# A second level of the seven-product scheme inside one block product, and layer statistics from accumulated sums

## The chip, the cores and the metric

The kernel runs on one core of a Trainium2 chip. A core has five engines that run at the same time and wait for each other through semaphores: TensorE (PE) multiplies matrices into PSUM, VectorE (DVE) and ScalarE (ACT) work on elements and can read PSUM, GpSimd (POOL) works on elements in SBUF alone, and SyncE (SP) issues the transfers (DMAs). Each engine works through its own list of instructions in order. The metric is the time of one execution on the device in microseconds (us), less is better. All data are float32.

## The reference

The input x has 128 graphs of 128 nodes with 512 features, and adj is one 128x128 matrix for all. Four layers follow each other, and each ends with the residual and a layer norm over the features:

```python
# --- layer 0: y = adj @ x;  out = y @ W0 + bias
x = _layernorm(x + _L0_gnn_ref(x, adj, weight, bias))
# --- layer 1: rel = adj.T * (q @ k.T), each row divided by its norm;  out = rel @ v
x = _layernorm(x + _L1_gnn_ref(x, adj, Wq, Wk, Wv))
# --- layer 2: attention with softmax of leaky_relu(s1 + s2) * adj;  elu(att @ h + beta * h), h = x @ W
x = _layernorm(x + _L2_gnn_ref(x, W, a, beta, adj))
# --- layer 3: for each node the greatest of relu(...) over the features
x = _layernorm(x + _L3_gnn_ref(x, adj, adj, b))
```

The layer norm is `(x - m) / sqrt(v + 1e-5)` with mean m and variance v of each node's 512 features.

## The kernel before, in words

The 128 graphs are taken in 32 groups g of four. For one group a layer's big product is [512 rows] x [512 x 512 weights]: y @ W0 in layer 0 (written `y`), x @ (Wq.T Wk) in layer 1 (written `m`), x @ Wv.T in layer 1 (`v`) and z @ W in layer 2 (`z`). There are four such products per group. Each is done by a Strassen-Winograd scheme: the operands are cut into 2x2 blocks of 256x256, seven block products P1 to P7 replace eight, and sums of blocks are made before and after. `left_factors` makes the sums of the left operand on POOL (tiles `s_y`, `s_x`, `s_z`), `weight_blocks` makes those of the weights once. A block product is four matmuls of 128x128 weights against 256 columns. A float32 matmul appears in the profile as two records, so a block product has eight.

`product` issues the seven in the order 1, 2, 6, 5, 7, 3, 4. Their sums are formed in PSUM as far as possible, in regions:

```python
ORDER = (1, 2, 6, 5, 7, 3, 4)
REGION = {1: 0, 6: 0, 7: 0, 4: 0, 2: 1, 5: 2, 3: 2}
BLOCK = {1: (0, 0), 2: (0, 0), 6: (0, 1), 3: (0, 1), 5: (1, 1), 7: (1, 1), 4: (1, 0)}
```

P1, P6, P7 and P4 are accumulated onto one another in region 0; after each of them the region's present value is read out (`out`) into the block that BLOCK names, and the next of them can begin only when that read is done. P5 and P3 share region 2 in the same way. P2 is alone in region 1 and is added to block (0, 0). For `m`, `v` and `z` the read-outs of 1, 6, 5 and 4 are copies on ACT, the others adds on DVE. For `y` all read-outs are adds on DVE, and ACT copies the bias into regions 0 and 2 beforehand (`fill`).

Between the block products stand smaller steps of PE, one after each of the first products: `aggregate` (p_y, adj @ x of the next group; ACT copies it to yT) in `m`, `scores` (p_rel) in `y`, `gather` (p_z; ACT copies it to zT) in `v`, and `widen` (p_a, read by DVE for the maximum, `mx`) and `attend` (p_o, read by DVE with the residual) in `z`. In PSUM region 0 has two banks, regions 1 and 2 share one bank, the small steps share three banks (`bank`), and two banks hold a constant (`wa`).

The order of the work is written out by hand. Every step is put on a list with a time (`emit(at, ...)`), where 28 units are one group's period; the list is sorted, and each engine gets its instructions in the order of that list (`keep_in_program_order`). TABLE gives the times of an ordinary group; FIRST and LAST give those of the first two and the last three. Four groups are in work at once. While `y` of group g runs, layer 2 of group g - 2 makes its attention: `leaky` (DVE, two operations on e), `weighted` (POOL, e times adj), `greatest` (DVE, nm), `exps` (ACT) and `divide` (DVE).

The statistics of layers 0, 1 and 2 are made by `stats`, a pair of DVE instructions (BATCH_NORM_STATS2 and BATCH_NORM_AGGREGATE) for each graph. `norm` turns them into scale and shift, and ACT applies these. Layer 3 of the ordinary groups already uses sums and ACT's squares.

All instructions are issued through one helper, so the profile puts them all on line L26. Groups are told apart by the names of their tiles.

Of the kernel before, what the change touches and what calls it, by code (L numbers as in the profile page):

```python
# [8 lines left out]
FP = mybir.dt.float32  # L9
# [20 lines left out]
def kernel(  # L30
# [52 lines left out]
    dram = ctx.enter_context(tc.tile_pool(name="dram", bufs=2, space=bass.MemoryType.DRAM))  # L83

    def bank(name):
        return psum.tile([P, D], FP, tag="ps", name=name, bufs=3)

    def on_all(row, n):

# [27 lines left out]

    w2_sb = const.tile([P, K, D], FP)
    nc.sync.dma_start(w2_sb, w2.rearrange("(k p) f -> p k f", p=P))
    a_sb = data.tile([P, 2, D], FP, tag="x3", name="a_sb")  # L120
    nc.sync.dma_start(a_sb.rearrange("p s d -> p (s d)"), on_all(a2, 2 * D))
    beta_sb = const.tile([P, 1], FP)
    nc.sync.dma_start(beta_sb, on_all(beta, 1))
# [33 lines left out]
    def weight_blocks(at, key, w, keep=0, tag=None):  # L157

        def blk(kh, ch):
            return w[:, 2 * kh : 2 * kh + 2, H * ch : H * ch + H]

        t = {}

        def factor(i):
            if i == 0:
                home, args = (const, {}) if tag is None else (data, dict(tag=tag))
                u = home.tile([P, 3 + keep, 2, H], FP, name=f"t_{key}", **args)
                t.update({2: u[:, 0], 3: u[:, 1], 4: u[:, 2]})  # L170
                t[1] = u[:, 3] if keep else blk(0, 1)
                bw[key] = {
                    1: blk(0, 0), 2: blk(1, 0), 3: blk(1, 1), 4: t[4], 5: t[1], 6: t[2], 7: t[3],
                }
            to, left, op, right = (
                (3, blk(1, 1), ALU.subtract, blk(0, 1)),
                (2, t[3], ALU.add, blk(0, 0)),
                (4, blk(1, 0), ALU.subtract, t[2]),
                (1, blk(0, 1), ALU.subtract, blk(0, 0)),
            )[i]  # L180
            dve.tensor_tensor(t[to], left, right, op)

        for i in range(4):
            emit(at[i], factor, i)

    bw = {}


    def prepare_v(c):
# [7 lines left out]
    def prepare_dots(k):  # L197

        for i in range(2):
            scr = work.tile([P, D], FP, tag="scr", name=f"scr_wa_{i}_{k}", bufs=2)  # L200
            dve.scalar_tensor_tensor(
                scr,
                w2_sb[:, k, :],
                1.0,
                a_sb[:, i, :],
                op0=ALU.mult,
                op1=ALU.mult,
                accum_out=col[:, i, k : k + 1],
            )
# [21 lines left out]
    def row(at, step, n=G):  # L231
# [4 lines left out]
        load=[-20], y=row(0.5, 1), y_sums=row(4.3, 0.5), y_w=row(7, 1, 7),  # L236
        stats0=row(14.4, 0.4), norm0=[16.2], apply0=row(16.8, 0.33),
        turn=row(21.4, 1), turn_blocks=row(18.4, 0.6),
        move=row(20.5, 0.1), x_sums=row(25.3, 0.5), m=row(28, 1, 7), scores=row(36.5, 1),
        masked=[39.95], squares=[40.4], turn_rel=[40.3],  # L240
        move_rel=row(41.2, 0.1), inverse=[42.5], v=row(42, 1, 7), attend=row(50.6, 1),
        residual=row(51.0, 1), dots=[51.7, 53.8, 54.9, 55.6], norm1=[54.6], scale=[57.2],
        apply1=row(65.4, 0.33),
        spread=[57.3], leaky=[62.6], weighted=[62.9], greatest=[63.9], exps=[64.0],
        divide=[65.2], turn_att=[68.6], with_beta=[69.0], turn_blocks_2=[65.7], move_2=[65.8], gather=row(71.5, 1),
        z_sums=row(75.3, 0.5), z_w=row(77, 1, 7), exp=[86.0, 87.0, 96.0, 99.6],
        elu=[86.4, 87.4, 96.8, 100.3], norm2=[101.4], apply2=row(102.4, 0.33),
        widen=[104.2, 104.9, 105.6, 106.3], top=[104.7, 105.4, 106.1, 106.8],
# [53 lines left out]
    REGION = {1: 0, 6: 0, 7: 0, 4: 0, 2: 1, 5: 2, 3: 2}  # L302
    BLOCK = {1: (0, 0), 2: (0, 0), 6: (0, 1), 3: (0, 1), 5: (1, 1), 7: (1, 1), 4: (1, 0)}

    def left_factors(at, s, aT, tag, name, keep):

        def blk(nh, kh):
            return s[aT][:, 2 * kh : 2 * kh + 2, 2 * P * nh : 2 * P * (nh + 1)]  # L310

        def first():
            sums = work.tile([P, 3 + keep, 2, 2 * P], FP, tag=tag, name=f"s_{name}")
            s1, s2, s4 = (sums[:, i] for i in range(3))
            s3 = sums[:, 3] if keep else blk(1, 0)
            s["f"] = {1: blk(0, 0), 2: blk(0, 1), 3: s4, 4: blk(1, 1), 5: s1, 6: s2, 7: s3}
            pool.tensor_tensor(s1, blk(1, 0), blk(1, 1), ALU.add)

        emit(at[0], first)
        emit(at[1], lambda: pool.tensor_tensor(s["f"][6], s["f"][5], blk(0, 0), ALU.subtract))  # L320
        emit(at[2], lambda: pool.tensor_tensor(s["f"][7], blk(0, 0), blk(1, 0), ALU.subtract))
        emit(at[3], lambda: pool.tensor_tensor(s["f"][3], blk(0, 1), s["f"][6], ALU.subtract))

    def by_rows(p, a, b, first):

# [21 lines left out]
                    skip_group_check=True,  # L347
                )

    def product(at, name, mul, s, w, c, fresh, begin=None, before=None, lead=0.7):  # L350

# [26 lines left out]
        def out(i):  # L380
# [3 lines left out]
            else:  # L384
                dve.tensor_tensor(dst, p, dst, ALU.add)

        for n, i in enumerate(ORDER):
            if before is not None and i in (1, 5):
                emit(at[n] - (0.7 if i == 5 else lead), fill, REGION[i])
            emit(at[n], step, i)  # L390
            emit(at[n] + 0.72, out, i)
# [9 lines left out]
        dve.bn_stats(st, t)  # L401
        dve.bn_aggr(s["mv"][:, b, :], st)

    def norm(at, apply_at, s, g, t):

        n = G // len(at)

        def spread(i):
            sl = slice(i * n, i * n + n)
            ve = small.tile([P, n], FP, tag=f"ve{n}", name=f"ve_{g}_{i}")  # L410
            dve.tensor_scalar(ve, s["mv"][:, sl, 1], EPS, None, op0=ALU.add)
            s["r", i] = small.tile([P, n], FP, tag=f"rstd{n}", name=f"rstd_{g}_{i}")
            pool.tensor_tensor(s["r", i], ve, mhalf[:, sl], ALU.pow)

# [23 lines left out]
    def layer0(g, t):  # L438
        s = {}

        def aggregate(b):
# [12 lines left out]
                s["yT"][:, :, b * P : (b + 1) * P], p.rearrange("p (k n) -> p k n", k=K)  # L454
            )

        if g > 0:
            emit(t["load"][0], load, g)
        each(t["y"], aggregate)
        left_factors(t["y_sums"], s, "yT", "s_yz", f"y_{g}", 0)  # L460
        product(
            t["y_w"],
            f"y_{g}",
# [4 lines left out]
            False,  # L468
            before=bias_halves,
            lead=4.4 if g == 0 else 0.7,  # L470
        )
        each(t["stats0"], lambda b: stats(s, f"0_{g}", b, x1[g][:, b, :]))
        norm(t["norm0"], t["apply0"], s, f"0_{g}", lambda: x1[g])
# [1 line left out]

    def layer1(g, t):
        s = {}

# [109 lines left out]
        def residual(b):  # L590
            if b == 0:
                x2[g] = data.tile([P, G, D], FP, tag="x2", name=f"x2_{g}")
            dve.scalar_tensor_tensor(
                x2[g][:, b, :],
                s["o", b],
                s["rn"][:, b : b + 1],
                x1[g][:, b, :],
                op0=ALU.mult,
                op1=ALU.add,
            )  # L600
            if g < NG - 1:
                stats(s, f"1_{g}", b, x2[g][:, b, :])


        def dots(b):
            if b == 0:
                s["d"] = small.tile([P, 2, G], FP, tag="d12", name=f"d12_{g}")
            for i in range(2):
                scr = work.tile([P, D], FP, tag="scr", name=f"scr_{g}_{b}_{i}", bufs=2)
                dve.scalar_tensor_tensor(  # L610
                    scr,
                    x2[g][:, b, :],
# [24 lines left out]
        else:  # L637
            each(t["turn_blocks"], turn_blocks)
            each(t["move"], move)
        left_factors(t["x_sums"], s, "xT", "s_x", f"x_{g}", 1)  # L640
        product(t["m"], f"m_{g}", by_columns, s, "m", middle_block, True, begin_middle)
        each(t["scores"], scores)
        emit(t["masked"][0], masked)
        emit(t["squares"][0], squares)
# [3 lines left out]
        else:  # L648
            emit(t["turn_rel"][0], turn_last)
        emit(t["inverse"][0], inverse)  # L650
        product(t["v"], f"v_{g}", by_rows, s, "v", rows_of(lambda: s["v"]), True, begin_values)
        each(t["attend"], attend)
        each(t["residual"], residual)
        if g == NG - 1:
            each(t["stats1"], lambda b: stats(s, f"1_{g}", b, x2[g][:, b, :]))
        each(t["dots"], dots)
        emit(t["scale"][0], scale_dots)
        norm(t["norm1"], t["apply1"], s, f"1_{g}", lambda: x2[g])

    s12 = {}  # L660

# [3 lines left out]
    def layer2(g, t):  # L665
        s = {}
        late = g >= NG - 2


        def spread():  # L670
# [61 lines left out]
            engine.tensor_tensor(e, e, rs[:, :, None].to_broadcast([P, n, P]), ALU.mult)  # L732

        def turn_att(i):
            if i == 0:
                s["p"] = bank(f"p_eT_{g}")
            for b in range(i * n, i * n + n):
                pe.transpose(s["p"][:, b * P : (b + 1) * P], s["e"][:, b, :], ident)

        def with_beta(i):  # L740
            if i == 0:
                s["eT"] = work.tile([P, G, P], FP, tag="eT", name=f"eT_{g}")
            dve.tensor_tensor(
                s["eT"][:, i * n : i * n + n, :],
                s["p"].rearrange("p (b n) -> p b n", b=G)[:, i * n : i * n + n, :],
                beta_b[:, i * n : i * n + n, :],
                ALU.add,
            )
# [57 lines left out]

        def elu(b):
            if b == 0:
                if g < NG - 1:
                    x3[g] = data.tile([P, G, D], FP, tag="x3", name=f"x3_{g}")  # L810
                else:
                    x3[g] = work.tile([P, G, D], FP, tag="xB", name=f"x3_{g}")
            x = x3[g][:, b, :]
            dve.scalar_tensor_tensor(
                x, s["c", b], 0.0, x2[g][:, b, :], op0=ALU.max, op1=ALU.add
            )
            dve.scalar_tensor_tensor(x, s["m", b], 1.0, x, op0=ALU.min, op1=ALU.add)
            stats(s, f"2_{g}", b, x)

        n = G // len(t["exps"])  # L820
        emit(t["spread"][0], spread)
# [10 lines left out]
            emit(t["move_2"][0], move)  # L832
        each(t["gather"], gather)
        if g < NG - 1:
            left_factors(t["z_sums"], s, "zT", "s_yz", f"z_{g}", 0)
            product(t["z_w"], f"z_{g}", by_rows, s, "2", rows_of(lambda: s["c"]), True, begin)
        else:
            each(t["z_w"], direct)
        each(t["exp"], exp)
        each(t["elu"], elu)  # L840
        norm(t["norm2"], t["apply2"], s, f"2_{g}", lambda: x3[g])

    def layer3(g, t):
        s = {}

        def widen(b):
            s["a", b] = bank(f"p_a_{g}_{b}")
            pe.matmul(s["a", b], adjT, x3[g][:, b, :], start=True, stop=True)  # L850


# [153 lines left out]
```

## Time and profile before

| | |
|---|---|
| median of 3 runs (lowest to highest) | 2173.91 us (2173.57 to 2174.77) |
| the profiled execution | 2173.83 us |
| its span, first to last instruction | 2172.0 us |
| granted TensorE clock | 0.996 |
| PE busy | 2149.1 us, 99% |
| DVE, ACT, POOL busy | 1560.6 us (72%), 1115.4 us (51%), 720.8 us (33%) |
| matmul records of 128x256: mean of one | 379 ns |
| matmul records of 128x128: mean of one | 275 ns |
| BATCH_NORM_STATS2 on DVE | x392, 685 ns |
| BATCH_NORM_AGGREGATE on DVE | x392, 182 ns |
| ACT square of 128x512 with its sum | 620 ns, and 190 ns to read the sum |
| POOL sum of 128x512 | 1270 ns |

The page of a profile gives busy times by engine, the chain of work that ended last, and groups of like instructions with their number, the mean of one, and the idle time before them. Matmuls and DVE and ACT instructions overlap with their successors, so the mean duration of one is longer than the time from one start to the next; the timeline, which lists instructions with their start, shows the latter.

### The profile page before, as it was taken

The page shows a single profiled execution, that of the slowest core. Times are in us where ns is not written, and L with a number is a line of the kernel's source. Part 1 is how long each engine was busy: PE and PEld are TensorE (multiplying, and loading weights), DVE is VectorE, ACT ScalarE, POOL GpSimd, SP SyncE. Part 2 cuts the span into 40 slices and gives each one's busy share as a digit, 9 for nine tenths or more (in the row PEclk, how much of TensorE's full clock was granted, in tenths as well). Part 3 has the DMA queues.
Part 4 walks back from the last instruction along what each step waited for, and adds up shares of the span by engine and source line. Part 5 has one row for each costly group of instructions (what it writes and reads, how often), then busy time and mean ns, then how long its engine had stood idle before and what let it go on. Part 6 is the DMA issues. An engine that isn't in the chain of part 4 may idle for free.

```text
span 2172.0 us, 31973 instructions
## 1 busy us (share of the span) xinstructions
PE 2149.1 (99%) x10887; PEld 1820.3 (84%) x10887; DVE 1560.6 (72%) x3429; ACT 1115.4 (51%) x2470; POOL 720.8 (33%) x589
## 2 busy tenths in 40 slices
PE   9999999999999999999999999999999999999996
PEld 8888888888888888888888888888888888888882
DVE  4667676776777776777777767767777767777677
ACT  3235545555545555455555455554455554555554
POOL 4223333333333233334233233323332333333331
PEclk9999999999999999999999999999999999999998
DMA  4012222322122322222222223222322222332201
GB/s 171 25 37 64 58 72 72 71 54 59 59 76 66 77 55 51 67 73 69 55 58 62 74 71 73 54 56 62 75 67 66 58 56 70 74 68 55 39 20 59
DMA packets 361970, 138.31 MB, mean 64 GB/s; under 512 B 303184, under 2 KB 318672, under 8 KB 361808
## 3 DMA queue, kind: packets, MB, share of 16 engines
q1 hardware_dynamic: 361280, 135.22, 24.8%
q8 instruction: 88, 1.44, 0.3%
q10 hardware_dynamic: 528, 1.05, 0.1%
q14 instruction: 74, 0.61, 0.1%
HBM read 55.12 MB, written 41.48 MB: 44 GB/s over the span
## 4 chain that ended last, share of the span: by engine, by line
PE 97%; DVE 2%; ACT 0%; POOL 0%; issue 0%; ACTq 0%; POOLq 0%; DVEq 0%
PE r_m L26 18%; PE r_y L26 18%; PE r_v L26 18%; PE r_z L26 17%; PE p_rel L26 5%; PE p_y L26 5%; PE p_o L26 5%; PE p_z L26 5%; PE p_a L26 5%; PE r_qk L26 1%; DVE st L26 1%; DVE x L26 0%; DVE mx L26 0%; PE first_r L26 0%; ACT x L26 0%; PE c L26 0%
## 5 line engine op out<-in xcount | busy, mean ns | idle before, releaser
L26 ACT ACTIVATE x<-x,nmean,rstd 128x512 f32<-128x512 f32 x384 | 285.4, 807 | 48.6 <-DVE nmean L26 45.1
L26 DVE BATCH_NORM_STATS2 st<-x 128x6 f32<-128x512 f32 x392 | 268.3, 685 | 9.7 <-ACT x L26 1.1
L26 POOL TENSOR_TENSOR rstd<-ve,mhalf 128x4 f32<-128x4 f32 (+1 forms) x99 | 109.3, 1104 | 340.3 <-DVE ve L26 340.3
L26 DVE TENSOR_TENSOR x<-r_y,x 128x512 f32<-128x512 f32 x224 | 152.4, 680 | 91.7 <-PE r_y L26 83.7
L26 ACT COPY yT<-p_y 128x512 f32<-128x512 f32 x128 | 74.9, 586 | 195.6 <-PE p_y L26 195.6
L26 DVE SCALAR_TENSOR_TENSOR scr<-x,wa 128x512 f32<-128x512 f32 x256 | 162.0, 679 | 0.0
L26 DVE TENSOR_REDUCE mx<-p_a 128x1 f32<-128x512 f32 x128 | 88.3, 690 | 99.6 <-PE p_a L26 96.8
L26 ACT ACTIVATE x<-x,mean,r 128x512 f32<-128x512 f32 x128 | 97.4, 808 | 113.9 <-DVE mean L26 112.4
L26 POOL TENSOR_TENSOR rn<-n,mhalf 128x4 f32<-128x4 f32 x32 | 32.6, 1017 | 358.3 <-ACT sq L26 358.3
L26 PEld LDWEIGHTS p_z<-eT,x 128*128 128x128 f32 x1024 | 133.8, 192 | 8.0 <-issue 0.9
L26 PEld LDWEIGHTS p_rel<-xT,tT 128*128 128x128 f32 x1024 | 134.0, 192 | 6.7 <-ACT tT L26 0.2
L26 PEld LDWEIGHTS p_y<-adjT,x 128*128 128x128 f32 x1024 | 133.6, 192 | 6.3
L26 ACT COPY tT<-r_m 128x512 f32<-128x512 f32 x128 | 75.6, 590 | 119.1 <-PE r_m L26 119.1
L26 DVE TENSOR_TENSOR tT<-r_m,tT 128x512 f32<-128x512 f32 x96 | 66.3, 691 | 96.9 <-PE r_m L26 94.2
L26 PE MATMUL p_rel<-xT,tT 128*128 128x128 f32 x1024 | 134.7, 275 | 0.0
L26 PE MATMUL p_z<-eT,x 128*128 128x128 f32 x1024 | 134.5, 275 | 0.1
L26 PE MATMUL p_y<-adjT,x 128*128 128x128 f32 x1024 | 134.1, 275 | 0.0
L26 POOL TENSOR_TENSOR s_y<-yT 128x512 f32<-128x512 f32 x32 | 40.6, 1269 | 281.1 <-ACT yT L26 281.1
L26 PE MATMUL p_a<-x,adjT 128*128 128x512 f32 x256 | 128.7, 606 | 5.1 <-ACT x L26 5.1
L26 ACT COPY zT<-p_z 128x512 f32<-128x512 f32 x128 | 73.7, 576 | 116.5 <-PE p_z L26 116.5
L26 PE MATMUL p_o<-v,relT 128*128 128x512 f32 x256 | 129.7, 592 | 0.0
L26 ACT COPY v<-r_v 128x512 f32<-128x512 f32 x128 | 74.2, 580 | 107.9 <-PE r_v L26 107.9
(157 smaller groups left out, 5218.7 us busy)
## 6 DMA issues: line engine op xcount, KB each, us to landing
out_dram<-x SPq DMA_DIRECT2D x128, 256.0 KB, 2.1
x<-in_x_dram SPq DMA_DIRECT2D x31, 1024.0 KB, 7.6
xT<-xB SPq DMA_DIRECT2D x480, 64.0 KB, 2.3
relT<-relB SPq DMA_DIRECT2D x496, 16.0 KB, 1.8
eBd<-eB SPq DMA_DIRECT2D x30, 256.0 KB, 2.0
eT<-eBd SPq DMA_DIRECT2D x120, 64.0 KB, 2.0
s<-s2d SPq DMA_DIRECT2D x29, 256.0 KB, 5.2
w_sb<-in_L_gnn_weight_dram ACTq DMA_DIRECT2D x1, 1024.0 KB, 6.0
```

The source lines that it names most:

```text
L26: return lambda *args, **kw: self.tc.keep_in_program_order(op(*args, **kw))
```

## The change

**One block product of the seven is itself done by seven.** P2 of a product multiplies a 256x256 block by a 256x256 block. It is cut into 2x2 blocks of 128x128, and seven matmuls of 128 columns (inner products 1 to 7) replace the four of 256. This is done in `y` for groups 2 to 31, in `m` and `v` for groups 1 to 30, and in `z` for groups 0 to 29. `inner_sums` makes four 128x128 sums of the left operand on POOL, `inner` those of the weights once. The seven go to quarters of a new PSUM bank (`pi`), again accumulated onto each other, and DVE adds them to block (0, 0) in seven adds of 128x128.

The six other block products and the inner ones are issued in the order that WITH_SMALL and SMALL give. To make room for the bank `pi`, the small steps share two banks instead of three. Scores and gather are issued one unit earlier.

**Statistics of layers 1 and 2.** In layer 1 (groups 0 to 29) and layer 2 (groups 0 to 28), the DVE instruction that makes the row also accumulates its sum, ACT squares the row and accumulates the squares, and `norm` takes mean and variance from the two sums with four small DVE instructions instead of one.

**Buffers.** x3 has one buffer instead of two, and so has the scratch tile of the dots. In the last groups some PSUM tiles are put into the banks `pi` and `r12`.

```diff
     def bank(name):
-        return psum.tile([P, D], FP, tag="ps", name=name, bufs=3)
+        return psum.tile([P, D], FP, tag="ps", name=name, bufs=2)
...
-        move=row(20.5, 0.1), x_sums=row(25.3, 0.5), m=row(28, 1, 7), scores=row(36.5, 1),
+        move=row(20.5, 0.1), x_sums=row(25.3, 0.5), m=row(28, 1, 7), scores=row(35.5, 1),
...
-        divide=[65.2], turn_att=[68.6], with_beta=[69.0], turn_blocks_2=[65.7], move_2=[65.8], gather=row(71.5, 1),
+        divide=[65.2], turn_att=[68.6], with_beta=[69.0], turn_blocks_2=[65.7], move_2=[65.8], gather=row(70.5, 1),
...
+        def inner_sums():
+            a = {
+                (j, k): s[aT][:, 2 + k, j * P : (j + 1) * P] for j in range(2) for k in range(2)
+            }
+            v = work.tile([P, 4, P], FP, tag=tag + "i", name=f"si_{name}")
+            s1, s2, s3, s4 = (v[:, i] for i in range(4))
+            pool.tensor_tensor(s1, a[1, 0], a[1, 1], ALU.add)
+            pool.tensor_tensor(s2, s1, a[0, 0], ALU.subtract)
+            pool.tensor_tensor(s3, a[0, 0], a[1, 0], ALU.subtract)
+            pool.tensor_tensor(s4, a[0, 1], s2, ALU.subtract)
+            s["fi"] = {1: a[0, 0], 2: a[0, 1], 3: s4, 4: a[1, 1], 5: s1, 6: s2, 7: s3}
+
+        if inner:
+            emit(at[3] + 0.01, inner_sums)
...
+    SMALL = (
+        (1.0, (1, 2), 1.3, (((0, 0), 1), ((0, 0), 0))),
+        (2.3, (6, 5), 2.6, (((1, 1), 2), ((0, 1), 0))),
+        (3.3, (7,), 3.8, (((1, 1), 0),)),
+        (4.9, (4, 3), 5.1, (((0, 1), 2), ((1, 0), 0))),
+    )
+    WITH_SMALL = {1: (0.0, 0.72), 6: (1.2, 1.95), 5: (2.4, 3.1), 7: (3.4, 4.3), 3: (5.0, 5.72), 4: (6.0, 6.72)}
+
+    def inner_product(at, name, mul, s, w, c):
+        columns = mul is by_columns
+        q = {}
+
+        def step(n):
+            if n == 0:
+                q["p"] = psum.tile([P, Q, P], FP, tag="pi", name=f"pi_{name}", bufs=1)
+            for i in SMALL[n][1]:
+                a, b = s["fi"][i], bw_inner[w][i]
+                pe.matmul(
+                    q["p"][:, {2: 1, 5: 2, 3: 2}.get(i, 0), :],
+                    b if columns else a,
+                    a if columns else b,
+                    start=(i == 1), stop=True, skip_group_check=True,
+                )
+
+        def out(n):
+            for (j, h), i in SMALL[n][3]:
+                dst = c(0, 0)
+                x, y = (h, j) if columns else (j, h)
+                dst = dst[:, x, y * P : (y + 1) * P]
+                dve.tensor_tensor(dst, q["p"][:, i, :], dst, ALU.add)
+
+        for n in range(len(SMALL)):
+            emit(at + SMALL[n][0], step, n)
+            emit(at + SMALL[n][2], out, n)
...
+        if inner:
+            inner_product(at[0], name, mul, s, w, c)
+            for i, (begins, ends) in WITH_SMALL.items():
+                if before is not None and i in (1, 5):
+                    emit(at[0] + begins - lead, fill, REGION[i])
+                emit(at[0] + begins, step, i)
+                emit(at[0] + ends, out, i)
+            return
         for n, i in enumerate(ORDER):
...
+    def square(s, g, b, x):
+        scr = work.tile([P, D], FP, tag="scr3", name=f"scr3_{g}_{b}")
+        act.activation(scr, x, AF.Square, accum_out=s["sq"][:, b : b + 1])
...
+            if from_sums:
+                m = small.tile([P, G, 1], FP, tag="mean", name=f"mean_{g}")
+                s["mv"] = m
+                m = m[:, :, 0]
+                dve.tensor_scalar(m, s["add"], 1.0 / D, None, op0=ALU.mult)
+                dve.tensor_scalar(
+                    s["sq"], s["sq"], 1.0 / D, EPS, op0=ALU.mult, op1=ALU.add
+                )
+                dve.scalar_tensor_tensor(ve, m, -1.0, m, op0=ALU.mult, op1=ALU.mult)
+                dve.tensor_tensor(ve, ve, s["sq"], ALU.add)
...
                 op0=ALU.mult,
                 op1=ALU.add,
-            )
-            if g < NG - 1:
+                **(dict(accum_out=s["add"][:, b : b + 1]) if summed else {}),
+            )
+            if g == NG - 2:
                 stats(s, f"1_{g}", b, x2[g][:, b, :])
...
-                    x3[g] = data.tile([P, G, D], FP, tag="x3", name=f"x3_{g}")
+                if g < NG - 2:
+                    x3[g] = data.tile([P, G, D], FP, tag="x3", name=f"x3_{g}", bufs=1)
```

## The prediction

> **What bounds the kernel now.** I read first the page: busy times and the chain that ended last.
>
> ```profile
> PE 2149.1 (99%) x10887; PEld 1820.3 (84%) x10887; DVE 1560.6 (72%) x3429; ACT 1115.4 (51%) x2470; POOL 720.8 (33%) x589
> ...
> PE 97%; DVE 2%; ACT 0%; POOL 0%; issue 0%; ACTq 0%; POOLq 0%; DVEq 0%
> ```
>
> TensorE (PE) sets the time: a microsecond of matmul saved is won, and a microsecond of PE waiting is lost in full. Next the timeline of one group in the middle, where every group repeats after 65.94 us (the first p_o at 1000.39 and at 1066.33).
>
> ```profile
> 1012.46 1.89 PE L26 MATMUL r_m<-xT,m_qk 128*128 128x256 f32 x8
> 1014.19 1.05 PE L26 MATMUL p_y<-adjT,x 128*128 128x128 f32 x8
> 1015.08 1.89 PE L26 MATMUL r_m<-xT,m_qk 128*128 128x256 f32 x8
> 1016.81 1.05 PE L26 MATMUL p_y<-adjT,x 128*128 128x128 f32 x8
> 1017.70 1.89 PE L26 MATMUL r_m<-s_x,t_m 128*128 128x256 f32 x8
> ```
>
> Columns: start, duration (pipelined end), operation. Start to start, a block product costs 1.728 us (8 records of 0.216) and a 128-column step 0.889 (8 of 0.111). 28 products, 12 such steps and 8 p_a/p_o of 0.86 make 65.9: PE has no gap. P1 of m is the first line, P2 the third, P6 the fifth. P6 accumulates onto P1's region, so it waits until ScalarE (ACT) has copied P1. The ACT timeline:
>
> ```profile
> 1015.28 0.58 ACT L26 COPY yT<-p_y 128x512 f32<-128x512 f32 x1 [2.03 <-PE p_y L26]
> 1015.76 0.59 ACT L26 COPY tT<-r_m 128x512 f32<-128x512 f32 x1
> ...
> 1033.80 0.57 ACT L26 COPY r_y<-bias_sb 128x512 f32<-128x512 f32 x1
> ...
> 1061.23 0.29 ACT L26 ACTIVATE top<-mx,b_sb 128x1 f32<-128x1 f32 x1 [0.93 <-DVE mx L26]
> ...
> 1065.01 0.56 ACT L26 COPY c<-r_z 128x512 f32<-128x512 f32 x1
> ```
>
> P1's copy stands behind p_y's own copy and ends at 1016.35, 2.16 us after P1 (1014.19). P6 is not due before 1017.70, since P2 and a second p_y stand between: they are the cover. The e chain, VectorE (DVE) then GpSimd (POOL):
>
> ```profile
> 1027.20 1.31 DVE L26 TENSOR_TENSOR e<-s,d 128x512 f32<-128x512 f32 x1
> 1028.55 1.59 DVE L26 SCALAR_TENSOR_TENSOR e<-e 128x512 f32<-128x512 f32 x1
> 1030.11 0.69 DVE L26 TENSOR_TENSOR x<-r_y,x 128x512 f32<-128x512 f32 x1
> 1031.53 0.69 DVE L26 TENSOR_REDUCE nm<-e 128x4 f32<-128x512 f32 x1 [0.73 <-POOL e L26]
> ```
>
> ```profile
> 1023.80 1.27 POOL L26 TENSOR_TENSOR s_y<-yT 128x512 f32<-128x512 f32 x1 [9.32 <-ACT yT L26]
> ...
> 1027.61 1.98 POOL L26 TENSOR_TENSOR s_y<-yT,s_y 128x512 f32<-128x512 f32 x1
> 1030.22 1.28 POOL L26 TENSOR_TENSOR e<-e,adj_sb 128x512 f32<-128x512 f32 x1 [0.63 <-DVE e L26]
> ```
>
> DVE waits for POOL's e before nm; ACT's exponentials follow, and behind them the bias copy (1033.80) that y's P5 needs. P5 starts at 1035.09, so the bias is 0.7 early.
>
> [...] e<-e takes 1.53 us against 0.68 for scr<-x,wa, whose wa lies in PSUM, and s_y<-yT,s_y 1.93 against 1.27. [...] The trace has granted clock 0.996; [...] so I keep it.
>
> **The change, part by part.**
>
> *Matmuls.* P2 (8 records, 1.728) becomes seven 128-block products, 14 records of 0.111 = 1.555: 0.173 us saved. y has it in groups 2 to 31, m and v in 1 to 30, z in 0 to 29: 120 times, 20.8 us, 0.69 per group.
>
> *DVE.* P2's one add (pitch 0.61) becomes seven of 128x128 from PSUM; the nearest row, eT<-p_eT,beta_i, has 0.29 alone. At 0.22 to 0.35 that is 1.2 us more for each product, 144 us in all. Removed: 236 statistics pairs at a pitch of 0.82 (1046.13 to 1046.95), 194 us. The sums ride on existing instructions: scr<-x,wa with its accumulator has pitch 0.61, like one without. The three more small operations in 59 norms cost some 0.15 each, 27 us. DVE stays level, with room (72%). The dots, now with a single scratch buffer, wait for each other, perhaps 0.1 each, eight per group; at about 1013 they end before the first inner add can start.
>
> *ACT.* 236 squares at a pitch of 0.61 (scr<-x) add 144 us to 1115: share 58%, not a bound by itself.
>
> *POOL.* 90 times four 128x128 operations of 0.43, each dependent one 0.08 later: 1.75 us a set, 158 us to 721.
>
> *Order.* The single adds and sums are cheap; what hurts is where P6 now stands. After P1 come one interleaved step and only two small products (0.445 us), then P6. Scores and gather were moved one slot earlier, and the PE order is P1, step, inner 1 and 2, P6, step, inner 6 and 5, P5, step, inner 7, P7, step, inner 4 and 3, P3, P4. The accumulating buffers stay as they were, so P6 still waits for P1's evacuation.
>
> 1. m. p_y ends (start to start) 0.889 after P1. ACT starts yT 0.20 later, tT 0.48 after that, 0.59 long: 1.27 after p_y, and about 0.06 for the signal. P6 is wanted 0.445 after p_y. Wait: 1.33 - 0.445 = 0.88. Behind P6 on PE stands everything. I add 0.05 for inner 7, which reaches its slot as DVE frees it: 0.93.
> 2. v. The same, since gather's p_z and its zT copy now precede v's P1 copy on ACT: 0.93, including 0.05 before inner 4 and 3, where DVE first waits for ACT's last square of layer 2.
> 3. z. Before: first p_a at 1059.44; its maximum lets ACT start top at 1061.23, and top, x, v, square, top, x, square, c follow without a gap; c ends 1065.57, 6.13 after p_a. The order of these eight on ACT is unchanged. P6 of z is wanted after p_a, p_a, P1, p_a (0.86 + 0.86 + 1.73 + 0.86) and 0.445 = 4.76. Wait with the signal: 1.45; the inner adds of v put 0.05 ahead of the maximum: 1.5.
> 4. y. P1's add is done 2.7 after y begins (1030.80 - 1028.12); P6 is wanted at 3.06: no wait. But the last p_y now ends 3.90 before y (inner 4 and 3, P3, P4) instead of 5.18, so POOL starts s_y at -3.05 instead of -4.32. [...] e-add -0.43 to 0.2, s_y third to 1.5, leaky to 2.15, s_y fourth to 3.4. Then the inner sums, 1.75, then e by adj, 1.27: nm starts at 6.45 (before 3.41). On DVE, behind nm, stand the adds of inner 1 and 2, done at 7.7; inner 6 and 5 are wanted on PE at 5.69 and wait until 7.75. The bias copy ends 2.84 after nm starts (1034.37 - 1031.53), at 9.3; P5 is wanted at 6.12 and starts at 9.35. Wait in all: 3.2.
>
> *PSUM and SBUF buffers.* General banks fall from 3 to 2. Reuse is two steps back: p_o's third needs its first one's residual, wanted 5 us later; maxima and copies of 0.6 to 0.7 fit too. In the tail four p_o in a row may lose 0.3. x3 with one buffer waits for the stores of the group before: SP issues these from 1007.62 to 1010.55, 2.1 us to landing, against the first elu write at 1017.69, about 5 us of cover; if it went, each lost microsecond would sit before inner 6 and 5 of m. eT's DMAs land about 18.4 after y begins, p_z needs them at 20.4; relT and xT have more than 5 us. SP's order is unchanged.
>
> **The sum.** Per group 0.93 + 0.93 + 1.5 + 3.2 = 6.56 lost, 0.69 won, net 5.87. Times 30: 176. The span is 2172.0 in an execution of 2173.83 us, 0.08 from the median of 2173.91, so 2173.9 + 176 = 2350. Bounds: m and v lie within 0.85 to 1.05, z within 1.35 to 1.7. [...] Net 4.5 to 7.1 per group, 2308 to 2387; start and tail, which I did not walk through, 5 either way.
>
> **Rivals.**
> - *The copies arrive in time (faster).* Then only the 20.8 us count: 2153. For it: ACT and DVE are idle for 49% and 28%, and ACT idles before 1015.28. Against: the idle time is waiting for p_y itself, and tT stands behind yT. It decides at 1.33 us after P1: tT directly behind P1 would end at 0.2 + 0.59 and be in time. 0.05.
> - *POOL's sums do not delay e (slower, less).* POOL is idle 9.3 us before s_y; if s_y starts early enough or the inner sums are very short, y's 3.2 vanish: 2173.9 + 30 x 2.67 = 2254. Against: that idle time is waiting for yT, whose last p_y comes later than before. 0.08.
> - *The waits feed each other or the clock drops.* Short waits all over might bring PE's clock below 0.996, or DVE, which waits in order for ACT's exponentials and squares, falls behind in m as well: 1.5 us more per group, 2395 or above. 0.09.
> - *The forecast:* 0.78.
>
> **How the numbers follow.** Predicted is the forecast's 2350. Its own bounds with the ends give 2300 to 2392; together with a part of the upper rival I take 2288 to 2397, which leaves out 0.18. Within 0.2% (4 us, about what a measurement of this kernel can tell from no change) would need gains and waits to balance by chance: 0.01. Faster 0.05, slower 0.94.
>
> **What would show it.** Waits of PE on ACT before r_m, r_v and r_z (third products), some 0.9, 0.9 and 1.5 us each, 30 times; PE waiting for DVE before p_i of y and for ACT's bias before r_y, together 3 us; POOL's e by adj directly behind four 128x128 operations; a period near 71.8 us; PE's sum of pitches lower by 21 us. A period near 65.3 would refute the walk; a period of 68.6 step 4 alone; a clock below 0.98 the assumption on it.

## The result, and the profile after

The changed kernel takes 2376.49 us (median of 4 runs, 2375.46 to 2377.59), the kernel before 2173.97 us on the same chip: a ratio of 1.0931, 95% interval 1.0912 to 1.095. The prediction was 2350, with a range of 2288 to 2397.

The page of the changed kernel, busy times and the chain that ended last:

```profile
PE 2184.8 (92%) x11607; PEld 1854.5 (78%) x11607; DVE 1518.3 (64%) x4106; ACT 1263.5 (53%) x2942; POOL 885.2 (37%) x949
...
PE 59%; ACT 22%; POOL 12%; DVE 4%; issue 2%; ACTq 0%; DVEq 0%; POOLq 0%
```

PE's share falls from 99% to 92%, and 34% of the chain has gone over to ACT and POOL. No engine is fuller than PE, so this is not a new engine as bound but PE waiting, in turn, for engines that are half idle. The view of PE's waits (what is waited for, us in total, times, longest) names the places:

```profile
PE pi_y L26 <- DVE x L26: 50.9, 30, 1.8
PE r_z L26 <- ACT c L26: 39.6, 29, 1.4
PE r_y L26 <- ACT r_y L26: 26.2, 31, 0.9
PE r_v L26 <- ACT v L26: 21.5, 30, 0.7
PE r_m L26 <- ACT tT L26: 21.0, 26, 0.8
```

In the kernel before, the same view has of these five only one:

```profile
PE r_y L26 <- ACT r_y L26: 0.3, 1, 0.3
```

Together the five are 159.2 us (the view leaves out waits of less than 0.15 us). They are the four steps of the prediction; y has two.

The timeline of one group (start, duration, operation, idle before it). First `m`; every group begins with it:

```profile
1107.22 1.89 PE L26 MATMUL r_m<-xT,m_qk 128*128 128x256 f32 x8
...
1108.94 1.05 PE L26 MATMUL p_y<-adjT,x 128*128 128x128 f32 x8
...
1109.84 0.61 PE L26 MATMUL pi_m<-xT,m_qk 128*128 128x128 f32 x4
...
1110.04 0.58 ACT L26 COPY yT<-p_y 128x512 f32<-128x512 f32 x1 [2.03 <-PE p_y L26]
1110.52 0.59 ACT L26 COPY tT<-r_m 128x512 f32<-128x512 f32 x1
...
1111.25 1.97 PE L26 MATMUL r_m<-s_x,t_m 128*128 128x256 f32 x8 [0.81 <-ACT tT L26]
```

P1 ends its issue at 1108.94. ACT is idle and could copy it, but the list has p_y's copy first, and p_y ends 0.9 later. So tT begins at 1110.52 and ends at 1111.11. P6, on the sixth line, is due at 1109.84 + 0.445 = 1110.285 and starts at 1111.25, 0.97 late. In the kernel before, P2 and a second p_y stood in this place.

Then y, from POOL's first sum of the left operand to P5:

```profile
1120.81 1.27 POOL L26 TENSOR_TENSOR s_y<-yT 128x512 f32<-128x512 f32 x1 [9.39 <-ACT yT L26]
...
1127.01 0.45 POOL L26 TENSOR_TENSOR si_y<-yT 128x128 f32<-128x128 f32 x1
...
1128.37 0.45 POOL L26 TENSOR_TENSOR si_y<-yT,si_y 128x128 f32<-128x128 f32 x1
...
1128.78 1.27 POOL L26 TENSOR_TENSOR e<-e,adj_sb 128x512 f32<-128x512 f32 x1
1130.08 0.69 DVE L26 TENSOR_REDUCE nm<-e 128x4 f32<-128x512 f32 x1 [3.54 <-POOL e L26]
1130.68 0.61 DVE L26 TENSOR_TENSOR x<-pi_y,x 128x128 f32<-128x128 f32 x2
...
1131.44 0.68 PE L26 MATMUL pi_y<-u,si_y 128*128 128x128 f32 x4 [1.74 <-DVE x L26]
...
1132.35 0.57 ACT L26 COPY r_y<-bias_sb 128x512 f32<-128x512 f32 x1
...
1132.98 3.13 PE L26 MATMUL r_y<-w_sb,s_y 128*128 128x256 f32 x8 [0.86 <-ACT r_y L26]
```

POOL makes the four inner sums from 1127.01 and only then e times adj. DVE stands 3.54 us before nm, with the adds of inner products 1 and 2 behind it, and PE behind these. ACT's exponentials follow nm, and the bias copy follows them, so PE waits a second time before P5.

The last line shows something else: P5 lasts 3.13 us where a block product lasts 1.89. In the traces of the kernel before and of the changed one, every change of the granted clock lies on one grid of edges 3.413 us apart. The view by stretches between such edges (length; busy time of PE, its weight loads, DVE, ACT and POOL, each with the number of instructions; granted PE clock; DMA share; GB/s):

```profile
1126.86:1130.27 3.41, 2.84 (x18) 2.44 (x17) 0.19 (x1) 0.00 (x0) 3.11 (x6) 1.00 0.00 0
1130.27:1133.69 3.42, 1.39 (x7) 1.18 (x8) 2.76 (x9) 2.13 (x9) 0.00 (x0) 1.00 0.00 0
1133.69:1137.10 3.41, 3.41 (x12) 2.90 (x12) 1.92 (x6) 3.16 (x5) 0.00 (x0) 0.50 0.20 77
1137.10:1140.51 3.41, 3.41 (x25) 3.20 (x24) 1.08 (x3) 0.29 (x1) 0.00 (x0) 1.00 0.31 82
```

The second stretch holds both waits of y, and PE works 1.39 us of it. In the third the granted clock is 0.50, for this stretch alone; such a stretch is called slow below. The first stretch has an idle part too, but a smaller one (3.41 - 2.84 = 0.57 us), and the stretch behind it has the clock at 1.00.

The period from one m to the next shows both effects. It is 72.18 us in most groups and 73.84 in eight of the last 28, those with such a slow stretch. A group of the mended kernel of experiment 8, which has none of these waits, takes 65.455 us. Set side by side, step by step, the undisturbed group that starts at 1181.07 is later by 1.04 in m (0.97 of waiting, and 0.07 by which the block product behind the wait takes longer: 1.80 to the next start, where 1.73 is usual), 3.09 in y (1.90, 1.09, 0.10), 0.97 in v (0.87, 0.10) and 1.60 in z (1.53, 0.07): 6.70 in all, of 72.18 - 65.455 = 6.73. Over the 28 periods the kernel before has 1849.3 us and the changed one 2034.8, 185.5 more; the first three periods give 14.4 and the rest lies in the ends.

### The profile page after: what moved, and what is told of

Its sections match the earlier page's. It is cut to its first block, busy times and chain, and to the rows that moved or that the text cites. A ratio compares the mean times of both kernels' runs of the same rounds, so it can differ in the third digit from the quotient of the medians.

```text
span 2375.8 us, 34753 instructions
## 1 busy us (share of the span) xinstructions
PE 2184.8 (92%) x11607; PEld 1854.5 (78%) x11607; DVE 1518.3 (64%) x4106; ACT 1263.5 (53%) x2942; POOL 885.2 (37%) x949
## 4 chain that ended last, share of the span: by engine, by line
PE 59%; ACT 22%; POOL 12%; DVE 4%; issue 2%; ACTq 0%; DVEq 0%; POOLq 0%
PE r_z L26 10%; PE r_y L26 10%; PE r_m L26 10%; ACT x L26 9%; PE r_v L26 8%; POOL s_y L26 5%; PE p_y L26 5%; PE p_o L26 4%; PE p_z L26 4%; ACT scr L26 3%; PE p_rel L26 3%; POOL yT L26 2%; POOL si_y L26 2%; ACT e L26 2%; ACT v L26 2%
## 5 line engine op out<-in xcount | busy, mean ns | idle before, releaser
L26 ACT ACTIVATE scr<-x 128x512 f32<-128x512 f32 x356 | 221.6, 622 | 83.3 <-DVE x L26 81.9
L26 DVE SCALAR_TENSOR_TENSOR x<-m,x 128x512 f32<-128x512 f32 x128 | 88.6, 692 | 165.5 <-ACT m L26 161.8
L26 DVE TENSOR_TENSOR x<-r_y,x 128x512 f32<-128x512 f32 x194 | 133.5, 688 | 79.1 <-PE r_y L26 75.4
L26 DVE SCALAR_TENSOR_TENSOR scr<-x,wa 128x512 f32<-128x512 f32 x256 | 174.8, 683 | 5.7
L26 PE MATMUL r_z<-t,s_z 128*128 128x256 f32 x496 | 119.7, 384 | 41.6 <-ACT c L26 39.6
L26 PE MATMUL r_y<-w_sb,s_y 128*128 128x256 f32 x512 | 132.2, 404 | 25.9 <-ACT r_y L26 25.9
L26 ACT ACTIVATE e<-e,nm 128x128 f32<-128x128 f32 x128 | 49.8, 390 | 186.8 <-DVE nm L26 186.8
L26 PEld LDWEIGHTS p_rel<-xT,tT 128*128 128x128 f32 x1024 | 140.6, 200 | 7.7 <-ACT tT L26 0.2
L26 PE MATMUL r_m<-s_x,t_m 128*128 128x256 f32 x512 | 124.1, 385 | 24.3 <-ACT tT L26 21.0
L26 PE MATMUL r_v<-t_v,s_x 128*128 128x256 f32 x512 | 124.2, 385 | 21.5 <-ACT v L26 21.5
```

The lines of the kernel that those rows point to most:

```text
L26: return lambda *args, **kw: self.tc.keep_in_program_order(op(*args, **kw))
```

## Experiments

The theory: the slowdown is made by the order of the work in the four products, each step by itself, and not by the arithmetic, the statistics or the buffers. The rivals: DVE or ACT has too much work, whatever the order; the two PSUM banks are too few; the PE clock has a part in it. Each ratio is to the kernel before, measured again beside the experiment; its medians there are 2174.34 to 2174.56 us.

**1. The statistics alone**, put into the kernel before.

```diff
...
-            )
-            if g < NG - 1:
+                **(dict(accum_out=s["add"][:, b : b + 1]) if summed else {}),
+            )
+            if g == NG - 2:
                 stats(s, f"1_{g}", b, x2[g][:, b, :])
...
-        norm(t["norm1"], t["apply1"], s, f"1_{g}", lambda: x2[g])
+        if summed:
+            each(t["squares1"], lambda b: square(s, f"1_{g}", b, x2[g][:, b, :]))
+        norm(t["norm1"], t["apply1"], s, f"1_{g}", lambda: x2[g], summed)
...
```

(The same in layer 2; `norm` works from the sums as in the changed kernel.)

> The kernel before with the statistics from sums and squares alone; no inner products, three general banks, the old order. Order theory (P6 ahead of P1's copy costs the time): PE's order is that of before, so 2174 to 2190 us; up to 0.5 us per group may be lost before p_a, since ACT has two squares more in v and its layer 2 norm ends only just in time there. Rival, the statistics cost the time (ACT's squares delay its copies): most of the 203 us, so above 2300.

Measured: 2170.77 us, ratio 0.9983 (0.9976 to 0.999), a little below what was expected. The period becomes 65.93, against a mean of 66.05 before. DVE's busy time falls from 1560.6 to 1373.3 us, ACT's rises from 1115.4 to 1264.5. The new statistics cost nothing: the periods of the kernel before vary from 65.93 to 66.27, and with the new statistics they stay at the lowest of these.

**2. Everything but the inner products**: the changed kernel with P2 whole and in its old place, with the old times of scores and gather, but with its two banks, single buffers and new statistics.

```diff
...
-        inner = g >= 2
+        inner = False
...
-        inner = 1 <= g < NG - 1
+        inner = False
...
-            left_factors(t["z_sums"], s, "zT", "s_yz", f"z_{g}", 0, not late)
+            left_factors(t["z_sums"], s, "zT", "s_yz", f"z_{g}", 0, False)
...
```

> The changed kernel with P2 as one block product in its old place, and scores and gather at their old times; two general banks, single buffers and the new statistics stay. Order theory: as the run with the statistics alone, 2174 to 2190 us. Rival, the two banks or the single buffers of x3 and scr cost the time: above 2250, and clearly above the run with the statistics alone.

Measured: 2174.27 us, ratio 0.9999 (0.999 to 1.0007), period 65.93 as in experiment 1. Against experiment 1 the banks and buffers cost 3.5 us once, in the ends (the first three periods are 0.65 longer), and nothing per group. So all of the loss is with the inner products and the order that they bring.

**3. The inner products alone**: the changed kernel with the old statistics.

```diff
-        summed = g < NG - 2
+        summed = False
...
-            if g == NG - 2:
+            if g < NG - 1:
                 stats(s, f"1_{g}", b, x2[g][:, b, :])
...
-        summed = g < NG - 3
+        summed = False
```

> The changed kernel with the old statistics in all layers, so the inner products, their order and the two banks alone. Order theory: the waits are those of the changed kernel, 2365 to 2400 us. Rival, the statistics cost the time: below 2250.

Measured: 2448.49 us, ratio 1.1257 (1.124 to 1.1274), outside what was expected and 72 us above the changed kernel. The view of PE's waits has the five of above nearly unchanged and two new ones:

```profile
PE pi_m L26 <- DVE tT L26: 22.0, 29, 0.8
PE pi_v L26 <- DVE v L26: 5.3, 29, 0.2
```

DVE's statistics stand between its adds of the inner products, and PE waits for the adds. That is 27 us. The clock does most of the rest: PE spends 118 us of the trace at half clock, against 46 in the changed kernel, which is 36 us more lost. The granted clock is 0.976, the period settles at 75.09 us, and every group has one slow stretch. The two parts of the change are thus not independent: the inner products need the DVE time that the new statistics set free. Experiment 9 tests this without the other waits.

**4. m and v: the copy of P1 ahead of p_y's and p_z's.**

```diff
             for i, (begins, ends) in WITH_SMALL.items():
+                if i == 1 and name[0] in "mv":
+                    ends = 0.45
```

> The changed kernel with P1's copy put ahead of the copy of p_y in m and of p_z in v on ACT, nothing else. Order theory: P1's copy ends 0.85 us after P1, P6 is wanted at 1.33, so the waits of r_m and r_v (1.05 and 0.98 us each with the restart, 30 times) go: 61 us less, about 2315, some 10 either way for the clock's windows. Rival, P6 waits for something else in m and v (its sums on POOL, the inner adds): less than 15 us won.

Measured: 2347.36 us, ratio 1.0795 (1.0779 to 1.0811). The waits of r_m and r_v are gone from the list, as expected, which should bring 30 x (1.04 + 0.97) = 60 us. So it was P1's copy that P6 waited for, and not its sums on POOL, to which the view of the changed kernel puts down four of the 30 waits in m: those sums are where they were. Half of the gain came, 29 us. From the fifth period on nearly all are 71.68 us, with this pair of stretches in each (columns as above):

```profile
1041.39:1044.80 3.41, 1.13 (x8) 0.78 (x7) 1.94 (x5) 1.85 (x9) 0.80 (x1) 1.00 0.00 0
1044.80:1048.21 3.41, 3.08 (x7) 2.52 (x8) 2.24 (x9) 2.40 (x4) 0.00 (x0) 0.50 0.08 32
```

71.68 us is 21 times 3.413. Without its slow stretch, taken at the 73.84 - 72.18 = 1.66 us that one cost in the changed kernel, a group would take about 70.02, 2.16 less than 72.18, where 2.01 was expected. So the step was understood, and the clock, granted at 0.977 in this run, took half of the gain: the group's length is now a whole number of stretches, and each group has a pair like the one shown.

**5. y: the inner sums on POOL behind e times adj.**

```diff
-            emit(at[3] + 0.01, inner_sums)
+            emit(at[3] + (1.11 if name[0] == "y" else 0.01), inner_sums)
```

> The changed kernel with y's four inner sums on POOL put behind e times adj, nothing else. Order theory: nm starts about 1.7 us sooner after y begins (6.4 to 4.7); behind nm the bias copy and the inner adds come sooner too, and y's waits fall from 3.0 to about 1.5 us. That is 45 us, and with less idle time in one stretch PE's clock should not be halved any more, some 15 us: about 2316. Rival, e is late for another reason [...]: less than 20 us won.

Measured: 2312.97 us, ratio 1.0635 (1.0621 to 1.065), as expected. The wait of pi_y for DVE is gone; the one for the bias stays (25.3 us, 30 times). The period is 70.47 and the granted clock 0.995: with the longest wait gone, no slow stretch is left between the first groups and the tail. This also decides what caused that wait: POOL has the same operations as before, only in another order, so it is the place of the four sums that makes it, and neither POOL's work nor, by itself, the later start of s_y or the two longer POOL operations beside e on DVE (1.98 and 1.72 us in the changed kernel).

**6. y entirely**: experiment 5, the bias copied ahead of the exponentials, and nm behind the first inner adds.

```diff
-        spread=[57.3], leaky=[62.6], weighted=[62.9], greatest=[63.9], exps=[64.0],
-        divide=[65.2], ...
+        spread=[57.3], leaky=[62.6], weighted=[62.9], greatest=[64.35], exps=[64.4],
+        divide=[65.65], ...
...
-                    emit(at[0] + begins - lead, fill, REGION[i])
+                    emit(at[0] + begins - (1.5 if i == 5 else lead), fill, REGION[i])
```

> As the run before, and in y also the first inner adds ahead of nm on DVE, the bias copy for P5 ahead of the exponentials on ACT, the second inner adds ahead of the division. Order theory: y's waits go but for 0.2 us, so 2.85 x 30 = 86 us and the 15 us of the clock: about 2275. Rival, P5 and the inner products of y wait for something else: above 2310.

Measured: 2272.47 us, ratio 1.0453 (1.0437 to 1.0469), as expected. y has no wait left, and the period is 69.14. What is later on DVE and ACT by this, the exponentials and the division, is waited for by nobody.

**7. z: the copy of P1 ahead**, between the squares of layer 3.

```diff
-        widen=[104.2, 104.9, 105.6, 106.3], top=[104.7, 105.4, 106.1, 106.8],
+        widen=[104.2, 104.9, 105.6, 106.3], top=[104.7, 105.52, 106.1, 106.8],
+        squares3=[104.1, 105.48, 105.54, 106.2],
...
+                if i == 1 and name[0] == "z":
+                    ends = 0.45
```

> The changed kernel with P1's copy of z ahead of the second square and second maximum of layer 3 on ACT (their times moved behind it), nothing else. Order theory: z's wait of 1.6 us goes, 47 us: about 2330 if the clock's windows keep hitting one group in three. If each period then meets a halved window at the same place, as in the run with m and v mended (period 71.68, 21 windows of 3.413), about 2347. Rival, z's P6 waits for other things: less than 15 us won.

Measured: 2370.89 us, ratio 1.0905 (1.089 to 1.092): 6 us won where 46 were expected. By the time alone the rival (less than 15 us) would have it. But the wait of r_z is gone, and the first full periods are 70.56 to 70.63, 1.6 below 72.18, so the step itself is worth what it should be. From the fifth period on they are 72.1 to 73.5. The granted clock is 0.971: the trace has 139 us at half clock, against 46 us in the changed kernel, which is 41 stretches against some 14. What PE won it lost again to its clock, and more completely than in experiment 4, where the granted clock was 0.977.

**8. All three edits** (4, 6 and 7 together).

```diff
+                if i == 1 and name[0] in "mvz":
+                    ends = 0.45
```

(The other lines are those of experiments 5, 6 and 7.)

> The changed kernel with all three edits: P1's copy first in m, v and z, and all of y's. Order theory: per group 0.69 us won and about 0.4 us of waits left (inner 7 in m, inner 4 in v, inner 6 in y, 0.1 each), clock as before: 2174 - 21 + 12 = 2165, between 2155 and 2180. Rival, an inner product of 14 short records costs more than one block product (weights change with each): not below 2190.

Measured: 2166.61 us (2165.04 to 2166.93), ratio 0.9962 (0.9949 to 0.9974), as expected. The page:

```profile
PE 2135.4 (99%) x11607; PEld 1832.7 (85%) x11607; DVE 1511.5 (70%) x4106; ACT 1270.2 (59%) x2942; POOL 885.8 (41%) x949
...
PE 95%; DVE 4%; ACT 1%; issue 0%; POOL 0%; ACTq 0%; DVEq 0%; POOLq 0%
```

The same instructions as in the changed kernel, with busy times on DVE, ACT and POOL within 7 us of its own, in another order: 210 us less, and 0.4% less than the kernel before. The period is 65.455. This excludes the rival that an engine has too much work, and the one that the inner product itself costs more than a block product. The steps together are worth more than one by one (29, 104 and 6 us in experiments 4, 6 and 7), since the clock, granted at 0.995, takes almost nothing back: one slow stretch is left between 100 and 2100 us.

Two things keep it above what the arithmetic promises. The saving is 65.93 - 65.455 = 0.475 us per group instead of 0.69: in m the inner product 7, and in v the inner product 4, still wait a little for DVE (0.10 and 0.09). And the start is longer. The timeline of PE in group 1, which runs its m behind group 0's attention:

```profile
103.99 0.46 PE L26 MATMUL pi_m<-si_x,u_m 128*128 128x128 f32 x2 [2.43 <-DVE d L26]
104.29 2.56 PE L26 MATMUL r_m<-s_x,t_m 128*128 128x256 f32 x8
```

PE waits 2.43 us for DVE, where an add stands behind the dots of group 0, and then has a slow stretch (the clock is 0.50 from 105.36 to 108.77, and the block product takes 2.56).

**9. The three edits with the old statistics.** The edit of experiment 3, on top of experiment 8:

```diff
-        summed = g < NG - 2
+        summed = False
...
-            if g == NG - 2:
+            if g < NG - 1:
                 stats(s, f"1_{g}", b, x2[g][:, b, :])
...
-        summed = g < NG - 3
+        summed = False
```

> The three edits together, but with the old statistics (bn_stats and bn_aggr on VectorE) in layers 1 and 2. If VectorE's statistics delay the adds of the inner products, as in the run of the inner products alone (0.8 us a group in m, 0.2 us in v), some 1.0 us x 30 = 30 us is lost against 2166.6: about 2190 to 2200 us, slower than before, and the new statistics are then what makes the inner products pay. The rival: with the waits of y, z, m and v mended VectorE has room for both, and the time is within 5 us of 2166.6.

Measured: 2217.11 us, ratio 1.0196 (1.0182 to 1.021): slower than the kernel before. The rival, that DVE has room for both, is out; the loss is larger than expected, 50 us. The granted clock is 0.997, so it is waiting and not the clock. The timeline of m in a group in the middle:

```profile
1030.90 0.69 DVE L26 BATCH_NORM_STATS2 st<-x 128x6 f32<-128x512 f32 x1
...
1036.61 0.62 DVE L26 TENSOR_TENSOR tT<-pi_m,tT 128x128 f32<-128x128 f32 x2
...
1037.37 0.68 PE L26 MATMUL pi_m<-si_x,u_m 128*128 128x128 f32 x4 [0.78 <-DVE tT L26]
...
1042.59 0.69 DVE L26 BATCH_NORM_STATS2 st<-x 128x6 f32<-128x512 f32 x1
1043.32 0.18 DVE L26 BATCH_NORM_AGGREGATE mv<-st 128x2 f32<-128x6 f32 x1
1043.42 0.26 DVE L26 TENSOR_TENSOR tT<-pi_m,tT 128x128 f32<-128x128 f32 x1
...
1043.73 0.49 PE L26 MATMUL pi_m<-xT,u_m 128*128 128x128 f32 x2 [0.21 <-DVE tT L26]
```

A layer 1 pair of statistics (BATCH_NORM_STATS2 and the BATCH_NORM_AGGREGATE behind it) at 1030.90 makes DVE late for the dots: the last of them starts 4.20 us after m, against 3.12 in experiment 8, and the first inner adds behind it follow 1.1 later. Inner 6 and 5 start 0.93 later than in experiment 8. A layer 2 pair at 1042.59 stands directly ahead of the next add, and PE is later by another 0.37 before inner 4 and 0.10 behind it. y and v add 0.59 and 0.36 in this group. It is one of the longer ones, of 68.02 us; 17 of the 28 take about 67.03, and in one of these y adds nothing, m 1.00, v 0.36 and z 0.21. That DVE's mean load is 76% says nothing of this: the add is needed at one moment, and there DVE is at a pair.

**10. The three edits, m's inner products only from group 2 on.**

```diff
-            t["m"], f"m_{g}", by_columns, s, "m", middle_block, True, begin_middle, inner=inner
+            t["m"], f"m_{g}", by_columns, s, "m", middle_block, True, begin_middle,
+            inner=inner and g > 1,
```

> The three edits together, with m's inner seven products only from group 2 on (in group 1, m's P2 is whole and in its old place). If m of group 1 waits behind group 0's dots, its wait of 2.4 us and the slow window behind it (1.7 us) go, and 0.2 to 0.9 us of work comes back: about 2162 to 2164 us. The rival: the start is set by VectorE's dots whoever waits for them, and the time stays at 2166.6.

Measured: 2163.25 us (2163.02 to 2163.6), ratio 0.9948 (0.9935 to 0.9962), as expected. The first three periods together are 176.6 us, 3.8 less than in experiment 8, and the others are the same to 0.1 in all. Both the wait and its slow stretch are gone. It is the fastest of all the kernels here, the one before and the changed one among them.

## Why the prediction was right, point by point

The predicted walk through one group held, wait by wait. The 26 us between 2350 and 2376 come from terms that were put too low or at nothing, and half of them from the clock.

- *What bounds the kernel*: right. A microsecond of PE waiting was lost in full; experiment 6 won 104 us, where y's waits are 30 x 3.09 = 93 and the eight slow stretches some 13.
- *Matmuls*, 0.69 us saved per group: the mended order has 0.475, with 0.19 in the two remaining waits for DVE. The prediction had put 0.05 for each of these.
- *DVE, ACT, POOL*: 1518 us, 1264 and 885 measured; POOL's four sums take 0.45 to 0.46 each where 0.43 was put. That figure was the author's estimate: the trace before has no POOL sum of 128 columns. No engine's work mattered. Experiment 9 shows that the removal of the pairs on DVE did, which the prediction had counted only as busy time.
- *Step 1 (m) and step 2 (v)*, 0.93 each: 1.04 and 0.97. The wait itself was put at 0.88 and was 0.97 and 0.87; in m PE starts 0.14 us after the copy's end, where 0.06, an estimate, was put. Left out was that the first product behind a wait took 0.07 to 0.10 longer. Experiment 4 confirms the cause, the copy of P1 behind the other copy.
- *Step 3 (z)*, 1.5: 1.53, and 0.07 for the restart. Experiment 7 confirms the cause by the periods before the clock sets in.
- *Step 4 (y)*, 3.2: 3.09. nm was said to start 6.45 after y, and starts 6.23 after it (1130.08 - 1123.85); P5 was said to start at 9.35 and starts at 9.13. In the timeline after, POOL's operations for the sums of y take 1.27 us alone, and 1.98 and 1.72 beside e on DVE (1.36 and 1.60). How long the two would hold each other up was the author's estimate; no experiment separates it.
- *PSUM and SBUF buffers*: right, nothing per group (experiment 2), some 3.5 us once.
- *The clock*: wrong, and with the restarts the reason for 2376 instead of 2350. The prediction kept the clock of 0.996 of the kernel before; that the short waits would leave it there was the author's estimate, and no trace had shown it: from 100 to 2100 us the kernel before has at most 0.10 us of idle time in any stretch of the grid. The changed kernel has nine slow stretches between 100 and 2200 us, one in the start and eight in the 28 periods, each behind a stretch with 1.75 to 2.03 us of idle time. The prediction's own sign, a clock below 0.98, would not have shown it: the clock was 0.991. Eight of the 28 periods pay 1.66 us, 13 us. The restarts of 0.07 to 0.10 in m, v, z and y, with the other small differences of the steps, make 6.70 instead of 6.56 per group, 4 us. The matmul saving fell 0.2 us short per group, of which the statistics gave 0.12 back: 3 us. The rest of the 26 us, some 6, lies in the start, which has a slow stretch of its own at 106 us, and in the tail; the prediction had allowed 5 us for these.
- *The rivals*: that the copies arrive in time is refuted by the five waits, and that POOL's sums do not delay e by the 3.54 us before nm (0.73 in the kernel before) and by experiment 5. "The waits feed each other or the clock drops" happened in a small way in the changed kernel, and in full in experiment 3, where DVE falls behind in m and the clock is at 0.976.

## What to carry to other kernels

When a product is cut finer, look first at what its old length had covered: here P2 and the step behind it had hidden the copy of P1, and a saving of 0.17 us in each product uncovered waits of 1 to 3 us. Then the order of the copies on the other engines is to be written anew, with what PE needs next ahead of the rest; the same instructions in another order took 2166.6 instead of 2376.5 us. And short waits are to be taken away together: here, while the others remained, the granted clock fell to 0.977 and 0.971 (experiments 4 and 7), and 29 us were won where 60 were expected, and 6 where 46 were.

## What the runs showed of the hardware

*Stretches at half clock.* Between 100 and 2200 us of the changed kernel, take each stretch of 3.413 us of the grid and subtract PE's busy time in it, as the view by stretches gives it. Nine stretches have the granted clock at 0.50, each for one stretch alone. The stretches ahead of these nine were at 1.00 and had 1.75 to 2.03 us of idle time; those at 1.00 with another at 1.00 behind them had at most 1.75. The longest single wait does not tell the two apart. Ahead of eight of the slow stretches it was 0.88 to 1.16 us, as in the stretch from 1348.73, where parts of y's two waits of 1.74 and 0.86 us make 1.75 in all. In the stretch from 693.37 one wait alone made the 1.75 us, and the stretch behind it was at 1.00. In experiment 4 the stretch from 1041.39 has 2.28 us of idle time, and in experiment 8 the one from 101.95 has 2.04; the one behind is at 0.50 both times. The kernel before has at most 0.10 us in any stretch from 100 to 2100 us, and its clock is at 1.00 throughout. The ends of matmuls are modelled in the profile, so these idle times belong to this way of counting. That the idle time makes the slow stretch is the author's reading; no run varied it alone.

*Two periods were whole numbers of stretches.* Experiments 3 and 4 have periods of 75.09 and 71.68 us, 22 and 21 times 3.413, with a slow stretch in each. Why the period settles there was not tested.

*The product behind a wait took longer.* In the changed kernel a block product behind a wait took 1.80 to 1.83 us to the next start, instead of 1.73 (m at 1185.11, y at 1206.82, v at 1220.23, z at 1239.13). The 128-column product behind the wait of 2.43 us in experiment 8 took 0.30 instead of 0.22.

*An accumulated sum took no DVE time of its own.* In the changed kernel the instruction that makes the row in layer 2 with its sum lasts 0.69 us (1118.36), as it does without the sum in the kernel before (1044.00). The next one starts 0.62 us after it, and the record that reads the sum (0.08 us) starts together with that one (both at 1118.98). With 236 such sums in place of as many pairs DVE's busy time falls by 187 us in experiment 1. But the dots, which share one scratch buffer in the changed kernel, stand 0.73 us apart there (1108.54 to 1109.27) instead of 0.61 in the kernel before (1012.64 to 1013.25).
